# An adaLN block with attention and routed experts: block order, stores of finished sums, and the order of the first loads changed

## The chip, the cores and the metric

One core of a Trainium2 chip runs the whole kernel as one program. The metric is the device time of that core in microseconds (us), the median of three runs; a smaller number is better. The core has a matrix engine (PE; its weight loads are listed as PEld), a vector engine (DVE), an activation engine (ACT), a general engine (POOL) and a queue engine (SP) that mostly issues transfers. Each works through its own list of instructions in order, and they meet at semaphores.

## The reference

The input is `x` of 4 batches of 512 tokens with 256 columns. What is computed, cut to what matters:

```python
mod = (silu(c) @ wmod).reshape(4, 6, 1, 256)
sa, ca, ga, sb, cb, gb = ...            # shift, scale and gate, twice
ga = (2*(ga >= 0) - 1) * maximum(abs(ga), 0.25)   # gb likewise
h = layernorm(x) * (1 + ca) + sa
x = x + ga * attention(h)               # 32 query heads and 8 key heads of width 8, causal
h = layernorm(x) * (1 + cb) + sb
# 16 experts, 4 per token: best 2 of 4 groups of experts, then best 4 in them,
# weights normalized to a sum of 1; one shared expert for every token
ffn = sum_e cw[:, e] * (swiglu(h @ up[e].T) @ down[e].T) + swiglu(h @ sup.T) @ sdown.T
return x + gb * ffn
```

## The kernel before, in words

The program has two parts, `attention()` and `ffn()`, and an order that a small planner in the file makes. `Plan` holds operations, each with an engine, an assumed cost, what it needs, buffers that it takes and gives (`hold`), and a due time. `Plan.next` takes at each step the operation that can start earliest by those costs, the due time breaking ties, and `go` emits its instructions. So the order of each engine's list is fixed when the program is built, and an engine whose next instruction waits holds up all behind it.

**Attention.** Each batch has four packs, each of two key heads with their eight query heads: 16 packs, numbered s. `norm1(b)` (line 666) normalizes a batch, turns it on PE, applies shift and scale on ACT, and calls `split` (725) for the projections of queries and keys. `split` writes each value as a sum of three bf16 parts and stores these to memory (`qd`, `kd`). `load(s)` (808) reads a pack back as `qx` (3 transfers) and `kx` (9 transfers). For packs 0 and 1 the key loads are issued by ACT, otherwise by SP. `unused(n)` (511) fills the three pairs of `qx` and `kx` buffers beforehand, on DVE. `row_max(s)` (834) multiplies queries and keys (L860), adds the mask (L868) and takes row maxima on DVE (L881, 22 units a pack). `shift(s)` (897) splits the maxima, turns them on PE (L920), copies them (`mrow`, L930), and SP writes them into spare rows of `qx` (L940). Only then can `pack(s)` (944) start on the scores (L1001): ACT's exponentials follow (L1013), POOL's causal selection (L1020) and the product with the values (L971). `modulation(b)` (571) makes the gates and the second shift and scale of one batch, spread over all partitions, in two groups of eight PE instructions (L580) with DVE and ACT behind them; there are eight such groups. `later_loads` (1383) fetches batches 1 to 3 of `x` and the weights of the shared expert; `blank_all` (1394) fills two accumulators `acc_d` and the spare rows of `rows_d`.

**Second norm and routing.** `after(b)` (1078) projects the attention's result and adds it to `x`. `norm2(b)` (1146) makes the second norm, the router and for each token four slots; POOL scatters its row into `rows_d`, which has one region for each expert (L1342).

**Experts.** `make_table` (314) makes from the counts of rows a table of at most 79 blocks of 128 rows: the first row of each (`row_i`) and its expert (`of_i`), expert after expert. Several DVE operations there have 79 by 16 elements on each partition (L345 to L369). `shared` (397) does the shared expert (PE L416 and L454), adding into `x_sb`. `block(j)` (1483) fetches 128 rows (SP L1493), turns them (PE L1504), multiplies by the expert's first matrix (PE L1524), then SiLU (ACT L1534) and product (DVE L1538, reading ACT's result), turns back (PE L1543), copies (DVE L1547), multiplies by the second matrix (PE L1552), scales by the row's weight (ACT L1562), and POOL scatters the result with addition into `acc_d[j % 2]` (L1565). `meta` (DVE L1514, L1517) takes the token and the weight of each row, the latter as a sum over 16 columns masked by `is_of`. `read` (388) loads a register from a table (SP and PE, L389).

**End.** When all blocks are planned, eight pairs of tiles of 128 by 512 are read from the two accumulators (L1613, by SP and ACT), added, multiplied by the gate and added to `x_sb` (DVE and POOL, L1618 to L1623), and stored (L1624).

Of the kernel before, what the change touches and what calls it, by code (L numbers as in the profile page):

```python
# [10 lines left out]
F32 = mybir.dt.float32  # L11
BF16 = mybir.dt.bfloat16
AF = mybir.ActivationFunctionType
ALU = mybir.AluOpType
# [22 lines left out]
CAP = B * S + P  # L37
NBLK = B * S * TOPK // P + E - 1
# [113 lines left out]
def kernel(  # L152
# [92 lines left out]
    tile_rows = steps_of("tile_rows", [P, B * NT], [[P, B * NT]])  # L245
    number = steps_of("number", [P, NBLK], [[1, NBLK]])
    expert = steps_of("expert", [P, E], [[1, E]])
    begin = steps_of("begin", [P, E], [[CAP, E]])

    free = const.tile([P, E], F32, name="free")  # L250
    nc.gpsimd.tensor_copy(free, begin)
# [59 lines left out]

    table = {}

    def make_table(pool, needs, due):
        t, n = table, NBLK

        def counts():

            rows = pool.tile([P, E], F32, name="rows", bufs=1)
            nc.vector.tensor_tensor(rows, free, begin, ALU.subtract)  # L320
            full = pool.tile([P, E, B * NT], F32, name="full", bufs=1)
            nc.vector.tensor_tensor(
                full,
                rows.unsqueeze(2).to_broadcast([P, E, B * NT]),
                tile_rows.unsqueeze(1).to_broadcast([P, E, B * NT]),
                ALU.is_gt,
            )
            t["blocks"] = pool.tile([P, E], F32, name="blocks", bufs=1)
            nc.vector.tensor_reduce(t["blocks"], full, AX.X, ALU.add)

        def starts():
            blocks = t["blocks"]
            earlier = pool.tile([P, E, E], F32, name="earlier", bufs=1)
            nc.vector.tensor_tensor(
                earlier, before, blocks.unsqueeze(1).to_broadcast([P, E, E]), ALU.mult
            )
            first = t["first"] = pool.tile([P, E], F32, name="first", bufs=1)
            nc.vector.tensor_reduce(first, earlier, AX.X, ALU.add)
            t["last"] = pool.tile([P, E], F32, name="last", bufs=1)
            nc.vector.tensor_tensor(t["last"], first, blocks, ALU.add)  # L340

        def of():

            t["gone"] = pool.tile([P, n, E], F32, name="gone", bufs=1)
            nc.vector.tensor_tensor(  # L345
                t["gone"],
                t["last"].unsqueeze(1).to_broadcast([P, n, E]),
                number.unsqueeze(2).to_broadcast([P, n, E]),
                ALU.is_le,
            )  # L350
            t["of"] = pool.tile([P, n], F32, name="of", bufs=1)
            nc.vector.tensor_reduce(t["of"], t["gone"], AX.X, ALU.add)

        def is_of():
            t["is_of"] = pool.tile([P, n, E], F32, name="is_of", bufs=1)
            nc.vector.tensor_tensor(
                t["is_of"],
                expert.unsqueeze(1).to_broadcast([P, n, E]),
                t["of"].unsqueeze(2).to_broadcast([P, n, E]),
                ALU.is_equal,  # L360
            )

        def base():

            nc.vector.tensor_tensor(
                t["gone"], t["is_of"], t["first"].unsqueeze(1).to_broadcast([P, n, E]), ALU.mult
            )
            t["row"] = pool.tile([P, n], F32, name="row_f", bufs=1)
            nc.vector.tensor_reduce(t["row"], t["gone"], AX.X, ALU.add)  # L369
            nc.vector.tensor_tensor(t["row"], number, t["row"], ALU.subtract)  # L370

        def rows():

            row, of = t["row"], t["of"]
            nc.vector.tensor_scalar(row, row, float(P), None, ALU.mult)
            nc.vector.scalar_tensor_tensor(row, of, float(CAP), row, ALU.mult, ALU.add)
            nc.vector.tensor_scalar(row, row, float(E * CAP), None, ALU.min)
            nc.vector.tensor_scalar(of, of, float(E - 1), None, ALU.min)
            for name in ("row", "of"):
                t[f"{name}_i"] = pool.tile([P, n], mybir.dt.int32, name=f"{name}_i", bufs=1)  # L380
                nc.vector.tensor_copy(t[f"{name}_i"], t[name])

        op = needs
        for f, cost in ((counts, 0.9), (starts, 0.9), (of, 2.8), (is_of, 1.4), (base, 2.8), (rows, 1.0)):
            op = plan.add("DVE", cost, f, needs=[op], due=due)
        return op

    def read(t, n, engine, top):
        return nc.values_load(  # L389
            t[0:1, n : n + 1],  # L390
# [97 lines left out]
    def attention():  # L488
        with ExitStack() as ectx:
# [21 lines left out]
            def unused(n):  # L511
                nc.vector.memset(kx[n], -1.0)
                nc.vector.memset(qx[n], 0.0)
# [10 lines left out]
            def fill(after_it):  # L524

                filled.append(plan.add("DVE", 2.7, lambda: unused(0), [after_it], -6.5))
                for n, t in enumerate(vaugs):
                    summed.append(
                        plan.add(
                            "POOL", 3.6, on_pool(lambda t=t: denominators(t)), [after_it], n - 6.5  # L530
                        )
                    )
# [8 lines left out]
            plan.free.update(PE=6.5, ACT=5.0, DVE=5.0, POOL=6.0, SP=4.0)  # L541

# [28 lines left out]
            def modulation(b, last, due):  # L571

                st = {}
                h1, h2 = hold("p1"), hold("p1")

                def project(parts):
                    st["p"] = ps1.tile([P, 2, D], F32, name="p1")
                    for w, part in enumerate(parts):
                        for k in range(KC):
                            nc.tensor.matmul(  # L580
                                st["p"][:, w, :],
                                lhsT=sct[:, k, b : b + 1].to_broadcast([P, P]),
# [5 lines left out]
                def sign():  # L588
                    st["sign"] = work.tile([P, 2, D], F32, name="ao")
                    nc.vector.tensor_scalar(st["sign"], st["p"], 0.0, 2.0, ALU.is_ge, ALU.mult)  # L590
                    nc.vector.tensor_scalar_add(st["sign"], st["sign"], -1.0)

                def size():
                    st["size"] = work.tile([P, 2, D], F32, name="ao")
                    nc.vector.tensor_tensor(st["size"], st["p"], st["sign"], ALU.mult)

                def gates():
                    nc.vector.scalar_tensor_tensor(
                        g_sb[:, b], st["size"], 0.25, st["sign"], ALU.max, ALU.mult
                    )  # L600

                def second():
                    nc.scalar.copy(m2_sb[:, b, 0, :], st["p"][:, 0, :])
                    nc.scalar.add(m2_sb[:, b, 1, :], st["p"][:, 1, :], 1.0)

                op = plan.add("PE", 1.7, lambda: project((2, 5)), [last], due(), takes=[h1])
                op = plan.add("DVE", 1.15, sign, [op], due())
# [55 lines left out]
            def any_bank(b):  # L663

                if b > 0:
                    return one_bank()
# [1018 lines left out]
```

## Time and profile before

| what | us |
|---|---|
| median of three runs | 753.69 |
| lowest and highest run | 751.95, 757.3 |
| the profiled execution | 746.31 |
| its span, first to last instruction | 744.4 |
| PE busy in the span | 651.1 |
| DVE busy | 455.6 |
| ACT busy | 317.4 |
| POOL busy | 346.2 |

The mean granted clock of PE was 0.946 of full speed. A profile is of one execution: starts and lengths below are of that one. A line of a chain or a timeline begins with start and length in us. A line by windows gives busy time of PE, PEld, DVE, ACT and POOL (with the number of instructions), then the granted clock of PE, the busy share of the transfer engines and the rate of transfers. A busy PE is not PE at its peak, since matmuls overlap and their ends are modelled; in the chain of work that ended last PE's matmuls appear at the pace at which they follow each other. "SPq" and "ACTq" are transfers being issued by that engine.

### The profile page before, as it was taken

To read this page: it belongs to the slowest core of one execution; us is meant where nothing else is said; L and a number is where in the kernel's file an instruction comes from. 1 tells how busy PE (TensorE), PEld (TensorE's weight loads), DVE (VectorE), ACT (ScalarE), POOL (GpSimd) and SP (SyncE) were. 2 spreads that over 40 slices of the span, in tenths; PEclk is the share of its full clock that TensorE was granted. 3 is DMA by queue.
4 is the path that set the end of the run, shared out by engine and by line. 5 is a ranking of instruction groups with operands and counts; after the bars stand their busy time and mean duration, and the time that the engine had idled before them with its cause. 6 is when DMAs were issued, how large, how long until landed. Compare 5 with 4: busy or idle time off the path is not lost.

```text
span 744.4 us, 12881 instructions
## 1 busy us (share of the span) xinstructions
PE 651.1 (87%) x4205; PEld 411.5 (55%) x4236; DVE 455.6 (61%) x1286; ACT 317.4 (43%) x557; POOL 346.2 (47%) x449
## 2 busy tenths in 40 slices
PE   5576999999999999999987897599999999999920
PEld 3343455555544554445443385488777777777710
DVE  4695868778888888787885056644333333333417
ACT  2103654575556654564655411022444444444400
POOL 4000222335257462673736643722566666556632
PEclk9787999999999999999999799799999999999965
DMA  4585211111133220332101196821576666666575
GB/s 135 128 253 198 72 27 41 42 42 47 29 100 102 65 64 13 108 102 57 42 11 55 63 300 200 205 69 30 96 110 110 109 110 110 102 108 110 66 188 186
DMA packets 54969, 74.51 MB, mean 100 GB/s; under 512 B 8024, under 2 KB 48056, under 8 KB 53752
## 3 DMA queue, kind: packets, MB, share of 16 engines
q1 hardware_dynamic: 37992, 51.99, 25.1%
q0 software_dynamic: 14448, 19.31, 16.0%
q10 hardware_dynamic: 2464, 2.39, 1.1%
q8 instruction: 35, 0.57, 0.3%
q14 instruction: 30, 0.25, 0.1%
HBM read 41.11 MB, written 32.16 MB: 98 GB/s over the span
## 4 chain that ended last, share of the span: by engine, by line
PE 66%; DVE 17%; DMA 6%; POOL 3%; issue 3%; ACT 2%; ACTq 0%; another core or an unknown queue 0%; SPq 0%; DVEq 0%; POOLq 0%
PE pu L1524 13%; PE py L1552 9%; PE pa L971 8%; PE pr L860 8%; PE p L1001 6%; DVE mx_s L881 6%; PE pu L416 5%; PE py L454 3%; PE pr L868 2%; PE pb L1543 2%; PE pt L1504 2%; DMA s<-acc_d 2%; PE p L580 1%; ACT ex L1013 1%; DMA kx<-kd 1%
## 5 line engine op out<-in xcount | busy, mean ns | idle before, releaser
L881 DVE TENSOR_REDUCE mx_s<-pr 128x1 f32<-128x384 f32 (+3 forms) x352 | 212.6, 635 | 52.6 <-PE pr L868 50.5
L1013 ACT ACTIVATE ex<-p 128x1024 f32<-128x1024 f32 (+1 forms) x192 | 163.2, 880 | 103.3 <-PE p L1001 77.4
L1020 POOL TENSOR_SCALAR_AFFINE_SELECT ex<-ex 128x256 f32<-128x256 f32 (+1 forms) x192 | 93.5, 493 | 180.2 <-ACT ex L1013 177.8
L1565 POOL DMA_INDIRECT acc_d<-y_b,token x79 | 123.0, 1556 | 77.2 <-DVE token L1514 32.3
L860 PE MATMUL pr<-kx,qx 125*128 125x384 bf16 (+3 forms) x512 | 125.2, 309 | 20.9 <-DVE mx_s L881 10.0
L1524 PE MATMUL pu<-up_sb,xt 128*128 x316 | 106.6, 460 | 0.0
L1001 PE MATMUL p<-qx,kx 128*128 128x384 bf16 (+3 forms) x481 | 92.0, 299 | 9.5 <-DMA qx<-mrow 6.5
L971 PE MATMUL pa<-ex,vaug 128*32 128x512 f32 (+3 forms) x1024 | 96.8, 450 | 2.5 <-POOL ex L1020 1.0
L860 PEld LDWEIGHTS <-qx 125*128 125x128 bf16 x512 | 47.0, 101 | 77.4 <-issue 49.7
L868 PE MATMUL pr<-seen,ident_h 128*128 128x128 bf16 (+2 forms) x352 | 88.5, 251 | 0.0
L1552 PE MATMUL py<-down_sb,at_b 88*128 x316 | 81.5, 379 | 1.2 <-DVE at_b L1547 1.2
L1342 POOL DMA_INDIRECT rows_d<-row,slot x64 | 64.2, 1003 | 25.7 <-DVE slot L1339 13.0
L1552 PEld LDWEIGHTS py<-down_sb,at_b 88*128 88x128 f32 x316 | 59.7, 189 | 21.9 <-ACT y_b L1562 1.7
L1538 DVE TENSOR_TENSOR a_b<-sg_b,pu 128x176 f32<-128x176 f32 x79 | 26.6, 337 | 71.7 <-ACT sg_b L1534 71.6
L1001 PEld LDWEIGHTS <-kx 128*128 128x128 bf16 x512 | 40.8, 98 | 40.9 <-issue 25.8
L1524 PEld LDWEIGHTS pu<-up_sb,xt 128*128 128x128 f32 x316 | 53.9, 190 | 16.7
L1562 ACT ACTIVATE y_b<-py,cw_b 128x256 f32<-128x256 f32 x79 | 37.4, 473 | 46.5 <-PE py L1552 46.5
L1547 DVE COPY at_b<-pb 88x256 f32<-88x256 f32 x79 | 33.2, 420 | 29.7 <-PE pb L1543 29.7
L1534 ACT ACTIVATE sg_b<-pu 128x176 f32<-128x176 f32 x79 | 25.1, 317 | 60.6 <-PE pu L1524 58.3
L416 PE MATMUL pu<-h2t,sup_sb 128*128 128x256 f32 (+1 forms) x192 | 48.2, 402 | 1.7 <-DVE a L436 1.7
L868 PEld LDWEIGHTS <-ident_h 128*128 128x128 bf16 x352 | 35.0, 99 | 22.8 <-issue 15.7
L416 PEld LDWEIGHTS pu<-h2t,sup_sb 128*128 128x128 f32 (+1 forms) x192 | 36.6, 193 | 9.8 <-DVE a L436 2.0
(176 smaller groups left out, 738.2 us busy)
## 6 DMA issues: line engine op xcount, KB each, us to landing
x<-rows_d SPq DMA_DIRECT2D x79, 136.5 KB
qx<-qd SPq DMA_DIRECT2D x48, 192.0 KB
up_sb<-in_up_t SPq DMA_DIRECT2D x8, 704.0 KB
acc_d<-blank SPq DMA_DIRECT2D x2, 2176.0 KB
qd<-pt SPq DMA_DIRECT2D x16, 192.0 KB
down_sb<-in_down_t SPq DMA_DIRECT2D x8, 352.0 KB
rows_d<-blank SPq DMA_DIRECT2D x17, 136.5 KB
x_sb<-in_x SPq DMA_DIRECT2D x4, 512.0 KB
```

What stands on the lines that cost most here:

```text
L416: nc.tensor.matmul(st["p"][:rows, w, :], lhsT=sup_sb[:, k, c0 : c0 + rows], rhs=h2t[:, k, c1 : c1 + half], start=(k == 0), stop=(k == KC - 1),
L860: nc.tensor.matmul(pr[:, h, :], lhsT=qx[s % 3][:QKZ, REP * j + r + h, ts(i, P)], rhs=kx[s % 3][:QKZ, j, :w], start=True, stop=False, skip_ ...
L868: nc.tensor.matmul(pr[:, :, w - P :], lhsT=ident_h, rhs=seen.unsqueeze(1).to_broadcast([P, n, P]), start=False, stop=True, skip_group_chec ...
L881: nc.vector.tensor_reduce(mx[s][:, i, c0 : c0 + n], st["pr"], AX.X, ALU.max)
L971: nc.tensor.matmul(st["pa"][32 * r : 32 * r + 32, c * P :], lhsT=vaugs[b % 2][:, c, SLOTS * n + j, :], rhs=exs[r], start=(j == 0 and c == ...
L1001: nc.tensor.matmul(pe[:, h, :], lhsT=kx[s % 3][:, j, ts(c, P)], rhs=qx[s % 3][:, REP * j + r + h, c * P :], start=True, stop=True,)
L1013: nc.scalar.activation(ex, st["pe"], AF.Exp, scale=qk_scale)
L1020: nc.gpsimd.affine_select(out=st["ex"][:, :, 0:P], in_=st["ex"][:, :, 0:P], pattern=[[0, n], [1, P]], base=0, channel_multiplier=-1, compa ...
L1342: dma = nc.gpsimd.indirect_dma_start(out=rows_d, out_offset=bass.IndirectOffsetOnAxis(ap=st["slot"][:, i, k : k + 1], axis=0), in_=st["row ...
L1524: nc.tensor.matmul(st["pu"], lhsT=st["xt"][:, k, :], rhs=up_sb[:, bass.ds(st["e"], 1), k, :].rearrange("p e f -> p (e f)"), start=(k == 0) ...
L1552: nc.tensor.matmul(st["py"], lhsT=st["at"][:, c, :], rhs=down_sb[:, bass.ds(st["e"], 1), c, :].rearrange("p e d -> p (e d)"), start=(c == ...
L1565: nc.gpsimd.indirect_dma_start(out=acc_d[j % 2], out_offset=bass.IndirectOffsetOnAxis(ap=st["token"][:, 0:1], axis=0), in_=st["y"], in_off ...
```

## The change

1. The start. `norm1` projects keys before queries and stores the first pack's keys first. The norm of batch 1 is planned directly behind batch 0's, before the first maxima, and takes the (still unused) score banks; its part of `x` is loaded at the start. The fills of `qx` and `kx` go from DVE to POOL. Keys of pack 1 are loaded by SP instead of ACT.
2. The gates. One `modulations` for all four batches, on 4 rows, in two groups of eight PE instructions as the profile counts them; the result goes to memory and is read back spread over all partitions (2 transfers of 1 MB). It is planned after the maxima of pack 0, and `later_loads` after those of pack 1; `blank_all` after those of pack 3.
3. `shift` issues the transfer of the maxima from ACT's queue, not SP's.
4. Blocks are numbered by the batch in which the first row of the block lies, then by expert. `make_table` works with one block on each partition: 25 small DVE instructions.
5. `meta` reads the block's expert into a DVE register and copies that one column, in place of the masked sum. The buffers of tokens go from 6 to 12, those of `y_b` from 5 to 8.
6. `end(b)`: when the last block that can hold rows of batch b is scattered, the sums of that batch are read, finished on DVE in six instructions between the blocks (each placed right behind a `copy_back`) and stored; so for batches 0 to 2. The scatters do not wait for these loads. Only batch 3 is left for the end, in four tiles of 128 by 256, on DVE alone.

Built, PE's list has before the first scores: batch 0's norm, batch 1's norm and projections, all of pack 0's maxima, and 38 of the 108 PE instructions (weight loads counted) of pack 1's. Before the change it had 64 of these 108, two groups of turns of batch 1, and no projection of it. On ACT's list the nine loads of pack 0's keys stand behind the first shift-and-scale of batch 1.

```diff
@@ make_table
-            t["gone"] = pool.tile([P, n, E], F32, name="gone", bufs=1)
-            nc.vector.tensor_tensor(
-                t["gone"],
-                t["last"].unsqueeze(1).to_broadcast([P, n, E]),
-                number.unsqueeze(2).to_broadcast([P, n, E]),
-                ALU.is_le,
-            )
...
+            gone, of, last = small("gone", [P, B * E]), small("of_v", [P, 1]), t["last"]
+            nc.vector.tensor_scalar(gone, last, number, None, ALU.is_le)
+            nc.vector.tensor_reduce(of, gone, AX.X, ALU.add)
...
@@ unused, fill
-                nc.vector.memset(kx[n], -1.0)
-                nc.vector.memset(qx[n], 0.0)
+                return [nc.gpsimd.memset(kx[n], -1.0), nc.gpsimd.memset(qx[n], 0.0)]
...
@@ modulation -> modulations
-                                lhsT=sct[:, k, b : b + 1].to_broadcast([P, P]),
+                                lhsT=sct[:, k, :],
...
+                def spread():
+                    nc.sync.dma_start(out=m_d, in_=mods)
+                    for t, at in ((g_sb, 0), (m2_sb, 2)):
+                        nc.sync.dma_start(
+                            out=t, in_=m_d[:, at : at + 2, :].unsqueeze(0).to_broadcast([P, B, 2, D])
+                        )
...
@@ norm1
+                    (wk_sb, NG * HD, kd, NPK * b, NPK, SLOTS),
                     (wq_sb[:, :, ts(0, P)], P, qd, NPK * b, n, PH),
-                    (wk_sb, NG * HD, kd, NPK * b, NPK, SLOTS),
...
@@ load
-                    engine, queue = ("SP", nc.sync) if s > 1 else ("ACT", nc.scalar)
+                    engine, queue = ("SP", nc.sync) if s > 0 else ("ACT", nc.scalar)
@@ shift
-                    "SP", 0.4, lambda: nc.sync.dma_start(out=qx[s % 3][QKZ:], in_=st["mrow"]),
-                    [op], due, gives=[mrow_hold],
+                    "ACT", 0.1, lambda: nc.scalar.dma_start(out=qx[s % 3][QKZ:], in_=st["mrow"]),
+                    [op], due, lag=2.5, gives=[mrow_hold],
@@ the plan of attention()
             norm1(0, Pace(-8.0, -4.0, 40))
-            filled += [
-                plan.add("DVE", 2.7, lambda n=n: unused(n), [stored[False, 0]], -3.0)
-                for n in (1, 2)
-            ]
             load(0)
+
+            norm1(1, Pace(-4.0, -1.6, 42))
             load(1)
-            later = plan.add("SP", 5.0, later_loads, [loaded[0][-1]], 0.0, lag=8.0)
-            plan.add("SP", 3.0, blank_all, [later, loaded[1][-1]], 1.0)
-            gates_made = loaded[1][-1]
-            due = Pace(0.5, 3.0, B * 6)
-            for b in range(B):
-                gates_made = modulation(b, gates_made, due)
             row_max(0)
             row_max(1)
+
+            gates_made = modulations(placed[0], placed[1], 1.5)
+            later = plan.add("SP", 4.0, later_loads, [placed[1]], 1.6, lag=8.0)
...
+                if s == 1:
+                    plan.add("SP", 3.0, blank_all, [placed[3]], 3.0)
@@ block
+            def which():
+                st["e_v"] = read(t["of_i"][j : j + 1, 0:1], DVE, E - 1)
+
...
-                junk = fp.tile([P, E], F32, name="junk")
-                nc.vector.tensor_tensor_reduce(
-                    junk, x[:, D + 1 :], t["is_of"][:, j, :], 1.0, 0.0, ALU.mult, ALU.add, st["cw"]
-                )
+                nc.vector.tensor_copy(st["cw"], x[:, D + 1 :][:, bass.ds(st["e_v"], 1)])
...
+                tc.declare_no_dep(dma.ins, group="sums", reason="finished rows")
@@ new: end(b, n, due), for batches 0 to 2
+            needs = [*puts[n - 2 : n], backs[n + 3]]
+            pace = iter(backs[n + 8 :])
...
+                    nc.vector.tensor_tensor(st[0], st[0], st[1], ALU.add)
...
+                    nc.vector.tensor_tensor(
+                        st[0], st[0], g_sb[:, b, 1:2, :].to_broadcast([P, half, D]), ALU.mult
+                    )
...
+                    nc.vector.tensor_tensor(st[0], st[0], x_sb[:, tiles, :], ALU.add)
...
+                op = plan.add("DVE", 0.81, add, [*op, next(pace)], due, gives=holds[1:])
+                op = plan.add("DVE", 1.05, gate, [op, next(pace)], due)
+                op = plan.add("DVE", 0.7, residual, [op, next(pace)], due)
+                plan.add("SP", 0.5, store, [op], due, lag=4.0, gives=holds[:1])
@@ the end of ffn()
-        for n in range(B * NT // half):
-            pair = [ep.tile([P, half, D], F32, name=f"s{n}_{i}") for i in range(2)]
+        for n in range((B - 1) * NT, B * NT):
+            pair = [ep.tile([P, D], F32, name=f"s{n}_{i}") for i in range(2)]
...
-            eng = nc.gpsimd if n % 2 == 0 else nc.vector
-            eng.tensor_tensor(s, s, x_sb[:, ts(n, half), :], ALU.add)
-            nc.sync.dma_start(out=out_r[:, ts(n, half), :], in_=s)
+            nc.vector.tensor_tensor(s, s, g_sb[:, B - 1, 1, :], ALU.mult)
+            nc.vector.tensor_tensor(s, s, x_sb[:, n, :], ALU.add)
+            nc.sync.dma_start(out=out_r[:, n, :], in_=s)
```

## The prediction

> **What bounds the kernel now.** I read the windows by stage first, then the chain of work that ended last inside each, then single timelines.
>
> ```profile
> core 0: us, PE busy (x) PEld busy (x) DVE busy (x) ACT busy (x) POOL busy (x), PEclk, DMA share, GB/s
> 31.00:67.80 36.80, 25.23 (x123) 15.28 (x124) 28.14 (x60) 4.07 (x6) 1.04 (x1) 0.78 0.84 256
> 67.80:422.00 354.20, 337.96 (x2729) 174.68 (x2759) 270.81 (x643) 201.37 (x272) 166.96 (x272) 0.99 0.20 55
> 422.00:474.00 52.00, 36.31 (x176) 29.58 (x177) 32.87 (x101) 6.93 (x16) 25.69 (x28) 0.86 0.75 228
> 501.00:713.20 212.20, 210.39 (x1007) 160.03 (x1005) 78.50 (x404) 92.83 (x240) 125.60 (x84) 1.00 0.61 95
> 713.20:744.40 31.20, 0.00 (x0) 0.00 (x0) 17.12 (x20) 0.00 (x0) 7.72 (x6) 0.50 0.70 210
> ```
>
> Two stages are PE's: attention from the first scores on (338 of 354 us busy) and the blocks (210 of 212). There only less PE work or a new wait moves the end. The other three have other limits: the start, the routing and the end, where PE does nothing for 31.2 us. The chain names these limits:
>
> ```profile
> 61.62 6.10 DMA qx<-mrow
> 70.75 1.72 PE p L734 x4
> 133.30 1.73 PE p L580 x8
> 469.48 1.48 DVE row_f L369
> 603.37 0.86 PE py L1552 x4
> 604.24 0.22 PE pb L1543 x2
> 604.46 0.22 PE pt L1504 x2
> 604.68 1.19 PE pu L1524 x4
> 722.97 6.11 DMA s<-acc_d
> ```
>
> The first scores wait for a transfer of 6.10 us; PE also does batch 1's projections and the gates inside attention; a DVE operation of 1.48 us ends the table; a block is PE alone, 0.86 + 0.22 + 0.22 + 1.19 = 2.49 us, 79 times; the end is loads of sums and DVE.
>
> **Start.** Row maxima of pack 0 begin at 31.0 (PE) and the first scores at 67.8; between, PE is busy 25.2 of 36.8 us at a clock of 0.78. The transfer that ends the wait was slow because the fills came just before on the same queue:
>
> ```profile
> 52.10 2.74 SPq L1396 DMA_DIRECT2D acc_d<-blank  x2
> 54.94 6.59 SPq L1400 DMA_DIRECT2D rows_d<-blank  x1
> ```
>
> After the change the fills are planned after pack 3's maxima, and the maxima leave on ACT's queue. Pack 0's keys now stand behind the first shift-and-scale of batch 1 on ACT, so I put the first row maxima at 33, 2 us later than now. They take 22 DVE units, 13.3 us (212.6 us over 16 packs), plus about 2.8 for four other DVE operations of batch 1's norm at 0.69 and 3.8 for its projections on PE: to 53. Splitting and turning the maxima about 1.6, their copy 0.57, issue 0.76 (SP's median) and landing about 2.0 (an estimate from small transfers outside the fills): scores at 58.2, -9.6 us. Bounds -5 (keys 5 us later still) to -13. Batch 1's extra 0.5 MB of `x` at the start is about 1.5 us at the 350 GB/s of the first loads, which end near 10; transfers are idle from 10 to 20, so it costs nothing unless the first weights wait behind it, then 1.5.
>
> **PE work leaving attention.** Batch 1's projections, 1.72 + 1.86 + 1.72 + 1.93 (L734 three times, L789 once) = 7.2, move before the first scores. Of eight gate groups five stood after 67.8 at about 1.74; two remain, so 3 x 1.74 = 5.2 go. Against that, 64 of the 108 PE instructions of pack 1's maxima were done before the scores and now 38: 0.24 of 4.7 us (10% of the chain over 16 packs), +1.1. Sum -11.3. At the least -8, if PE waits where this work stood.
>
> **Transfers that pile up.** The spread of the gates (2 MB) and `later_loads` (about 2.4 MB) stand on SP just ahead of the last three key loads of pack 3, `blank_all` (4.4 MB) ahead of the last loads of pack 5. Now 67.8 to 422 moves only 55 GB/s. At 256 GB/s the first pile is 17 us, the second 17; a pack's PE time is about 22, and maxima run about a pack ahead. I take +5 of 0 (loads that far ahead) to +10 (one pile half bare). Issuing the maxima on ACT holds its exponentials 0.76 us, 16 times = 12.2; ACT is busy 201 of 354, so I count +2, bounds -1 (PE waited 6.5 us in all for this transfer) to +5. The fills of `qx` on POOL precede its first selection and are hidden there; bare they are about 2 us. Attention after 67.8: -11.3 + 5 + 2 = -4.3.
>
> **Table.** L345 to L369 run 461.2 to 472.4, 11.2 us, and PE waits for it:
>
> ```profile
> 473.24 1.22 PE L454 MATMUL py<-sdown_sb,a 96*128 96x256 f32 x2 [8.98 <-DVE a L436]
> ```
>
> `a` is an ordinary DVE product queued behind the table. The new table is 25 operations, no larger than 128 by 64; neighbouring operations of that size pace 0.25 and of 128 by 16 0.20: 13 x 0.25 + 12 x 0.20 = 5.65. So -5.6, and PE's 9 us wait lets it through; bounds -4 and -7.
>
> **Blocks.** PE's list per block is unchanged. DVE gets two things. First, reading the expert into a DVE register, in place of the masked sum (0.16 + 0.08). DVE loads no register from a table now; the nearest rows are those of PE and SP:
>
> ```profile
> L389 SPq TENSOR_LOAD <-row_i x79: 262/270/547, 477.4 to 686.9; - x79
> L389 PEldq TENSOR_LOAD <-of_i x79: 296/302/572, 490.2 to 702.2; - x79
> ```
>
> Second, 18 operations of `end` behind a `copy_back`, 0.69 each alone. The room for them:
>
> ```profile
> 603.76 0.34 DVE L1538 TENSOR_TENSOR a_b<-sg_b,pu 128x176 f32<-128x176 f32 x1 [1.18 <-ACT sg_b L1534]
> 604.50 0.42 DVE L1547 COPY at_b<-pb 88x256 f32<-88x256 f32 x1 [0.40 <-PE pb L1543]
> ```
>
> From the copy's end (604.92) the next product could start at 606.25: 1.33; PE's turn came 0.14 after the product's end, so 1.47 in all. Into it go meta's 0.23, the load 0.30 and in 18 blocks 0.69: 1.22. The load is short and hidden; if it drains DVE, what is late is the next product, then `pb` on PE. The Trainium skill ("DMA: Bandwidth & Descriptors", Latency and other measured facts) gives a floor of about 0.6 us for such a load; the two rows here show half. By the rule end-op blocks need 0.69 + 0.23 + 0.60 = 1.52, over by 0.05: 18 x 0.05 = 0.9 us; by the row nothing. From below it is 0, since PE paces; from above, the load's dependency (the DVE register use) is unknown. I take +1 of 0 to +6. SP now issues the loads of sums and stores too: 12 + 6 issues at up to 0.92 (a fetch unthrottled) within 212 us, against a fetch that runs several blocks ahead: nothing, or about one block, 2.5, if a fetch is late. The larger pools only loosen waits.
>
> A rule speaks against `end`: the skill ("SBUF — State Buffer", Who interferes with whom) says that a DVE instruction with two SBUF inputs and a POOL instruction that reads SBUF keep each other out for the whole instruction. The end of the run agrees, POOL's scatter does not:
>
> ```profile
> 729.79 1.63 DVE L1619 TENSOR_TENSOR s<-s,g_sb 128x512 f32<-128x512 f32 x1
> 649.08 1.56 POOL L1565 DMA_INDIRECT acc_d<-y_b,token  x1 [1.73 <-DVE a_b L1538]
> 649.72 0.16 DVE L1517 CUSTOM_DVE_ANT_0 junk<-x,is_of 128x16 f32<-128x16 f32 x1
> ```
>
> Beside POOL's addition, L1619 takes 1.63 and not 0.69; but L1517, two SBUF inputs, took its usual 0.16 in the middle of a scatter. By the rule each end operation would take about 1.69: (1.69 + 0.23 + 0.30 - 1.47) x 18 = +13.5; by the row 0. I take the row, and keep the rule as a rival.
>
> **End.** Now: last scatter issued 713.90 to 715.45, SP's loads issued at 717.74, first sum 722.93, last DVE operation over at 740.87, end 744.4 (3.5 for the store). Four times less has to be loaded: 1 MB, landed about 2.5 after issue (an estimate; 6.11 for the first of 4 MB), so 720.2. Twelve DVE operations of 128 by 256 at 0.40 (0.69 halved, plus start) = 4.8, no POOL beside them: 725.0, store 3.3: 728.3. That is -16; bounds -14 to -18.5.
>
> **Sum.** -9.6 - 4.3 - 5.6 + 1 - 16 = -34.5. The span goes from 744.4 to about 709.9. The profiled run took 746.31, 1.9 more than its span, and the median shown, 753.69, is 7.4 above that run. I take this distance as unchanged and subtract from the median: 719.
>
> **Rivals.** *B, attention gives it all back:* batch 1's norm ahead of the first maxima makes the keys late, or the piles stop PE at packs 3 and 5. For it: the keys' place on ACT's list, 8.8 MB moved into a dense stage. Against: 55 GB/s there now. Then only end, table and blocks count: 753.7 - 16 - 5.6 + 1 = 733. *C, end operations shut out by the scatter,* as priced above: 719 + 13.5 = about 732. For it the 1.63 row, against it the 0.16 row. *D, on the other side: the register load on DVE.* The windows have 1.47 - 0.23 = 1.24 us for it in every block. If DVE must empty and fetch before the copy that uses the register, a load of L costs (L - 1.24) x 79. It eats the whole gain at 1.24 + 34.5/79 = 1.68 us; at 2.0 it costs 60: 779. For it: no DVE load is in the trace[...]. Against: 0.27 and 0.30 on two other engines. *E, all pays in full:* piles and ACT's issue cost nothing, the start gives 13: about 707.
>
> **How the numbers follow.** Forecast 0.60, B 0.17, C 0.07, D 0.12 (a third within 1%, the rest slower), E 0.04. About 1% (7.5 us) is what a measurement of this kernel can tell from no change. Faster by over 1% is the forecast, B, C and E: 0.88; within 1% 0.04; slower 0.08. The forecast's own range is 707 to 731, its bounds added in part; 705 to 738 takes in B and C and leaves out D and the far ends of B and E, about 2 in 10.
>
> **What would show it.** In the changed kernel's profile: the first L1040 scores near 58 (start); a window from there to the last pack some 4 us shorter than 354, with PE's waits for `kx` and `qx` loads at packs 3 and 5 of at most 5 us; PE's wait for `a` near 3 rather than 9; a block still at 2.49 us on the chain, with DVE's register load near 0.3; L1660 and L1663 at 0.7 between blocks; 15 us from the last block's PE work to the end rather than 31. Wrong would be a row maximum that starts after 38, a DVE load over 1.2 us, block intervals over 2.55, or a chain in attention that runs through transfers.

## The result and the profile after

| | before | after |
|---|---|---|
| median, us | 752.55 (20 runs) | 759.6 (20 runs) |
| ratio | 1 | 1.0118, interval 1.0088 to 1.0149 |
| the profiled execution | 746.31 | 763.72 |
| its span | 744.4 | 762.0 |

Slower by 1.2%; forecast was 719. The two profiled executions lie 6 under and 4 over their medians, so the 17.6 us between their spans overstates the 7 us between the medians. The stages below come from these single executions; what a change is worth is taken from the ratios of the experiments. (Ratios and intervals leave disturbed runs out.)

The windows of the changed kernel, cut at its own first row maxima, first scores, end of attention, first all-block stretch and last PE work:

```profile
core 0: us, PE busy (x) PEld busy (x) DVE busy (x) ACT busy (x) POOL busy (x), PEclk, DMA share, GB/s
37.80:64.35 26.55, 20.60 (x98) 10.95 (x97) 21.12 (x39) 5.11 (x9) 0.00 (x0) 0.74 0.32 80
64.35:441.70 377.35, 335.61 (x2688) 167.71 (x2720) 270.68 (x639) 196.11 (x260) 167.90 (x272) 0.96 0.26 74
441.70:531.00 89.30, 72.45 (x303) 57.66 (x304) 38.31 (x137) 11.06 (x27) 35.24 (x41) 0.83 0.54 165
531.00:740.90 209.90, 208.69 (x1001) 158.98 (x999) 85.64 (x346) 93.27 (x240) 123.42 (x82) 1.00 0.66 118
740.90:762.00 21.10, 0.03 (x1) 0.00 (x0) 4.83 (x12) 0.47 (x1) 5.79 (x4) 0.59 0.49 103
```

| stretch | before | after | difference | predicted |
|---|---|---|---|---|
| to the first scores | 67.8 | 64.35 | -3.4 | -9.6 |
| first scores to the last pack's result | 354.1 | 377.35 | +23.2 | -4.3 |
| from there to PE's last work | 290.7 | 299.2 | +8.5 | -4.6 |
| PE's last work to the end | 31.8 | 21.1 | -10.7 | -16 |

Attention is where most of the time went. PE is busy there 335.6 us of 377.35, against 338 of 354.1 before: its idle time rose from 16.1 to 41.7 us, and the work that is left, less than before, ran at a mean granted clock of 0.96 (0.99 before) and took nearly as long. The chain of work that ended last now runs through transfers there:

```profile
83.43 3.35 DMA qx<-mrow
92.38 3.66 SPq L1425
98.17 8.36 DMA sdown_sb<-in_sdown_t
133.80 4.98 DMA qx<-mrow
141.70 6.95 SPq L1437
152.46 3.75 DMA kx<-kd
```

L1425 is in `later_loads`, L1437 in `blank_all`. On SP they stand ahead of the last three key loads of packs 3 and 5, which are issued from 101.6 and from 150.0 on. PE's waits between 64 and 165 us name what came of it (line, what it waited for, us in total, times, longest):

```profile
PE pr L898 <- DMA sdown_sb<-in_sdown_t: 6.3, 1, 6.3
PE pr L898 <- DMA kx<-kd: 4.3, 1, 4.3
```

L898 makes row maxima, and reads no `sdown_sb`: the wait is put down to a transfer that stood ahead of its keys. The first wait is for pack 3's keys, the second for pack 5's; the expectations below count them as packs 2 and 4. Pack 3's first products stand on PE's list in the midst of pack 1: when the wait begins, at 100.3, a quarter of pack 1's scores is still to come behind them. The start, on ACT's timeline:

```profile
29.21 2.25 ACTq L860 DMA_DIRECT2D kx<-kd  x6
31.51 0.78 ACT L710 ACTIVATE ht<-p,mod_t 128x512 f32<-128x512 f32 x1 [1.60 <-DMA kx<-kd]
40.44 0.58 ACT L765 CAST pt<-p 128x512 bf16<-128x512 f32 x1 [5.51 <-DMA kd<-pt]
```

ACT's key loads hold the second shift-and-scale of batch 1 for 1.60, and ACT then waits 5.51 for a store of keys to land before it can write another `pt`. PE's first product for row maxima comes at 37.8; DVE takes its first maximum at 41.66, behind a subtraction that waited for this `pt`, 3.8 us after PE (1.05 before). The first scores come at 64.35.

### The profile page after: what moved, and what is told of

Same layout as the page of the kernel before. It is cut to its first block, busy times and chain, and to the rows that moved or that the text cites. A ratio compares the mean times of both kernels' runs of the same rounds, so it can differ in the third digit from the quotient of the medians.

```text
span 762.0 us, 12858 instructions
## 1 busy us (share of the span) xinstructions
PE 661.2 (87%) x4155; PEld 407.5 (53%) x4188; DVE 439.0 (58%) x1206; ACT 314.9 (41%) x551; POOL 355.0 (47%) x450
## 4 chain that ended last, share of the span: by engine, by line
PE 63%; DVE 16%; DMA 8%; issue 4%; SPq 3%; POOL 3%; ACT 3%; ACTq 0%; DVEq 0%; POOLq 0%
PE pu L1558 12%; PE py L1586 9%; PE pa L1010 7%; PE pr L898 7%; DVE mx_s L919 6%; PE pu L416 5%; PE p L1040 5%; PE py L454 3%; PE pr L906 3%; PE pt L1538 2%; PE pb L1577 2%; DMA qx<-mrow 2%; PE p L1161 2%; ACT ex L1052 2%; DMA acc_d<-y_b,token 2%
## 5 line engine op out<-in xcount | busy, mean ns | idle before, releaser
L1599 POOL DMA_INDIRECT acc_d<-y_b,token x79 | 124.8, 1580 | 84.2 <-DVE token L1551 26.1
L898 PE MATMUL pr<-kx,qx 125*128 125x384 bf16 (+3 forms) x512 | 126.5, 311 | 22.4 <-DVE mx_s L919 8.9
L1040 PE MATMUL p<-qx,kx 128*128 128x256 bf16 (+3 forms) x479 | 93.3, 302 | 11.2 <-DMA qx<-mrow 7.5
L898 PEld LDWEIGHTS <-qx 125*128 125x128 bf16 x512 | 46.9, 102 | 84.0 <-issue 60.9
L1381 POOL DMA_INDIRECT rows_d<-row,slot x64 | 62.6, 979 | 25.8 <-DVE slot L1378 13.1
L416 PE MATMUL pu<-h2t,sup_sb 128*128 128x256 f32 (+1 forms) x192 | 52.6, 430 | 9.1 <-issue 5.4
L416 PEld LDWEIGHTS pu<-h2t,sup_sb 128*128 128x128 f32 (+1 forms) x192 | 38.6, 205 | 18.8 <-issue 5.8
```

What stands on the lines that cost most here:

```text
L416: nc.tensor.matmul(st["p"][:rows, w, :], lhsT=sup_sb[:, k, c0 : c0 + rows], rhs=h2t[:, k, c1 : c1 + half], start=(k == 0), stop=(k == KC - 1),
L898: nc.tensor.matmul(pr[:, h, :], lhsT=qx[s % 3][:QKZ, REP * j + r + h, ts(i, P)], rhs=kx[s % 3][:QKZ, j, :w], start=True, stop=False, skip_ ...
L1040: nc.tensor.matmul(pe[:, h, :], lhsT=kx[s % 3][:, j, ts(c, P)], rhs=qx[s % 3][:, REP * j + r + h, c * P :], start=True, stop=True,)
L1381: dma = nc.gpsimd.indirect_dma_start(out=rows_d, out_offset=bass.IndirectOffsetOnAxis(ap=st["slot"][:, i, k : k + 1], axis=0), in_=st["row ...
L1599: dma = nc.gpsimd.indirect_dma_start(out=acc_d[j % 2], out_offset=bass.IndirectOffsetOnAxis(ap=st["token"][:, 0:1], axis=0), in_=st["y"], ...
```

## The experiments

Theory A: attention's own changes make the loss, above all the transfers moved onto SP's queue. Rival R: the experts' side makes it. Ratios are to the kernel before, with intervals; milestones in us are of each kernel's profiled execution.

**Which half.** `e1_old_attention` keeps only the parts 4 to 6 of the change, `e2_old_experts` only the parts 1 to 3. `e3_fills_early` is the changed kernel with

```diff
             load(1)
+            later = plan.add("SP", 5.0, later_loads, [loaded[0][-1]], 0.0, lag=8.0)
+            plan.add("SP", 3.0, blank_all, [later, loaded[1][-1]], 1.0)
             row_max(0)
...
-            later = plan.add("SP", 4.0, later_loads, [placed[1]], 1.6, lag=8.0)
...
-                    plan.add("SP", 3.0, blank_all, [placed[3]], 3.0)
```

and `e4_no_register`, which has no operation that loads the register, with

```diff
-                nc.vector.tensor_copy(st["cw"], x[:, D + 1 :][:, bass.ds(st["e_v"], 1)])
+                nc.vector.tensor_copy(st["cw"], x[:, D + 1 : D + 2])
```

> Attention as before the change, table, blocks, sums and end as after it. Theory A (the loss is made in attention, where the span after stands 20 us behind when the last pack ends, and the experts' side gains a little: 31.2 to 22.7 at the end, 6 given back between attention and the first blocks): 2 to 8 us under the kernel before, ratio 0.990 to 0.998. Rival R (the loss is made on the experts' side by DVE's register loads, the slow queues around 490 to 505 and late scatters): over the kernel before, ratio 1.005 or more.

> Attention as after the change, table, blocks and end as before it. Theory A: attention ends some 20 us later than before, ratio 1.020 to 1.030, end of 31 us as before. Rival R: 0.985 to 1.000.

> The changed kernel, but later_loads and blank_all planned behind the first key loads as before the change; all else as changed. Theory A1 (the two piles on SP's queue at packs 2 and 4, 6.3 and 4.3 us of PE waiting for keys and the lower clock after them, are the main part of the loss in attention): 10 to 17 us under the changed kernel, ratio to the kernel before 0.990 to 1.000, attention's end about 428 rather than 442. Rival A2 (the start and ACT's queue make the loss): ratio 1.008 to 1.02, since the fills now delay the keys and the first maxima.

> The changed kernel without the register load on DVE: the weight of a row is copied from a fixed column, so each row is weighted by the first expert's weight rather than its own expert's. Theory A: as the changed kernel, ratio to the kernel before 1.006 to 1.014, since PE paces the blocks. Rival R (the DVE loads stall SP, PE and ACT around 490 to 505, 10 us): ratio 0.995 to 1.003, SP's 16 fills of blank rows back at 15 us from 26.

| kernel | ratio | first scores | last pack | PE's last work | span |
|---|---|---|---|---|---|
| before | 1 | 67.8 | 421.9 | 712.6 | 744.4 |
| after | 1.0118 | 64.35 | 441.7 | 740.9 | 762.0 |
| e1 | 0.9881 (0.9836 to 0.9926) | 67.2 | 419.7 | 716.4 | 738.4 |
| e2 | 1.0279 (1.0225 to 1.0334) | 64.6 | 442.1 | 738.5 | 771.9 |
| e3 | 0.9924 (0.9901 to 0.9947) | 65.4 | 424.9 | 718.3 | 739.2 |
| e4 | 1.0131 (1.0084 to 1.0177) | 64.3 | 439.9 | 737.5 | 759.0 |

The experts' half is faster by 1.2%, attention's half slower by 2.8%. R falls; leaving out the register load gains nothing. Putting the moved transfers back gives 1.0118 - 0.9924 = 1.9%, about 14.6 us. In the two profiles the packs shrink by 17.9 us with the same PE work in them. The row of e3:

```profile
65.40:424.90 359.50, 329.10 (x2688) 165.40 (x2720) 269.87 (x638) 196.20 (x260) 168.02 (x272) 0.99 0.24 72
```

PE is idle 30.4 us there and not 41.7, and busy 6.5 us less, at a clock of 0.99 and not 0.96. So about a third of what the piles cost goes with a lower clock: between 100 and 120 us, around the first wait, it is 0.75 in the changed kernel and 1.00 in e3.

**What is left in attention.** e3 still needs 359.5 us from first scores to last pack, 354.1 before, though less PE work is in it. `e5_maxima_on_SP` is e3 with the maxima on SP's queue, `e7_gates_in_one` is e1 with `modulations` in place of the four `modulation`.

```diff
-                    "ACT", 0.1, lambda: nc.scalar.dma_start(out=qx[s % 3][QKZ:], in_=st["mrow"]),
-                    [op], due, lag=2.5, gives=[mrow_hold],
+                    "SP", 0.4, lambda: nc.sync.dma_start(out=qx[s % 3][QKZ:], in_=st["mrow"]),
+                    [op], due, gives=[mrow_hold],
```

> The kernel of e3_fills_early with the maxima issued on SP's queue again. In e3 attention still takes 359.5 us from first scores to last pack against 354.1 before, with 30 us of PE idle against 16, part of it waits for the maxima (5.7) and for POOL's selections behind them (4.7). Theory A3 (ACT's queue makes the maxima late): 4 to 8 us under e3, ratio to before 0.982 to 0.988. Rival A4 (the PE work taken out was the filler at the ends of packs, so the waits come whatever the queue): within 2 us of e3, ratio 0.990 to 0.996.

> The kernel of e1_old_attention with only the gates of the change: one modulations for all batches, planned behind the key loads of pack 1 as the first gates were before. It takes 6 groups of PE, about 10 us, out of attention. Theory A4 (PE work in attention is filler, the chain of maxima paces it): e1 within 3 us, ratio 0.985 to 0.992. Rival A5 (attention is bound by PE, each us of PE work counts): 5 to 10 us under e1, 0.975 to 0.982.

Measured: e5 1.0020 (1.0000 to 1.0040), e7 0.9959 (0.9939 to 0.9979), both outside every expectation on the slow side. The milestones say why: first scores at 76.4 in e5 and 75.9 in e7. In e5 the maxima of pack 0 stand on SP behind the fills, in e7 2 MB of gates came on top of them. What was to be tested shows behind that: e5's packs take 354.0, 5.5 less than e3's; e7's 348.8 (75.9 to 424.7) against e1's 352.5, 3.7 less. Of e1's eight gate groups five, about 1.74 us each, lie in this stretch, of e7's none: 8.7 us less work. So it seems that the maxima on ACT gain at the first pack and lose at the others. `e12_only_first_on_ACT` is e3 with

```diff
-                    "ACT", 0.1, lambda: nc.scalar.dma_start(out=qx[s % 3][QKZ:], in_=st["mrow"]),
-                    [op], due, lag=2.5, gives=[mrow_hold],
+                    "ACT" if first else "SP", 0.1 if first else 0.4,
+                    lambda: queue.dma_start(out=qx[s % 3][QKZ:], in_=st["mrow"]),
+                    [op], due, lag=2.5 if first else None, gives=[mrow_hold],
```

where `first` is `s == 0` and `queue` ACT's for it, SP's otherwise.

> The kernel of e3_fills_early with the maxima of pack 0 on ACT's queue, all later ones on SP's. e3 has first scores at 65.4 and 359.5 us of packs, e5 76.4 and 354.0. Theory Q (ACT's queue helps only where fills stand on SP's, and costs 5.5 us in the packs): both gains, 5 to 6 us under e3, ratio to before 0.983 to 0.987. Rival (the packs' length follows from when they start): e3 within 2 us, 0.990 to 0.995.

0.9785 (0.9748 to 0.9823): 1.4% under e3, about 10 us, twice what was expected. First scores 64.9, packs 348.3, against 359.5. PE's waits in the packs, of e3 and then of e12:

```profile
PE p L1040 <- DMA qx<-mrow: 6.5, 7, 1.9
PE pa L1010 <- POOL ex L1059: 4.7, 6, 0.9
```

```profile
PE p L1043 <- DMA qx<-mrow: 2.7, 3, 1.0
PE pa L1013 <- POOL ex L1062: 1.7, 2, 1.2
```

11.2 us over 15 packs is 0.75 each; one issue holds ACT 0.73 to 0.76. The sizes agree, but `lag=2.5` also changes the planner's order, and no run tells ACT's time from that order. (e13 and e14 below have the attention of e12 and a third fill. Their packs take 352.9 and 352.1, with one wait of 4.9 and 3.2 for pack 1's maxima, which stand on SP behind the fills; but for that wait they agree with e12.)

**The end.** `e6_all_sums_last` is e1 with all sums read at the end, as before. `e8_three_sums` is e1 with a third accumulator:

```diff
-                    out=acc_d[j % 2],
+                    out=acc_d[j % 3],
```

with the third load and addition that it needs in `end` and at the end.

> The kernel of e1_old_attention with the sums of all four batches read and finished at the end, as before the change; table and blocks as changed. Theory A: the end goes back from 22 to 31 us and scatters no longer fall behind (5 us); e1 plus 5 to 10 us, ratio to before 0.996 to 1.002. Rival (loads and stores between blocks gave nothing net): e1 within 2 us, 0.986 to 0.991.

> The kernel of e1_old_attention with three accumulators in turn rather than two, so that a scatter waits for the third before it. In e1 the last scatter is issued 6.9 us after PE's last work. Theory S (the wait for the scatter two before makes the lag): last scatter within 2.5 us of PE's last work, 3 to 5 us under e1, less about 1 for a third load and addition at the end: ratio 0.982 to 0.986. Rival (POOL's own 1.56 us and the transfers' rate make it): e1 or up to 2 us over, 0.988 to 0.992.

e6: 1.0045 (1.0024 to 1.0067), 1.6% over e1, and 31.7 us from PE's last work to the end against 22.0: `end` is worth about 12 us, a little over what was expected. In e6 the last scatter follows its row's weighting by 0.9 us, in the changed kernel it comes 5.7 late. The last scatter of the changed kernel (POOL) and the weighting that it belongs to (ACT):

```profile
740.97 0.47 ACT L1596 ACTIVATE y_b<-py,cw_b 128x256 f32<-128x256 f32 x1 [1.45 <-PE py L1586]
747.17 1.56 POOL L1599 DMA_INDIRECT acc_d<-y_b,token  x1 [0.76 <-DMA acc_d<-y_b,token]
```

The same two in e8:

```profile
722.82 0.47 ACT L1562 ACTIVATE y_b<-py,cw_b 128x256 f32<-128x256 f32 x1 [1.67 <-PE py L1552]
723.57 1.55 POOL L1565 DMA_INDIRECT acc_d<-y_b,token  x1 [0.58 <-ACT y_b L1562]
```

The row of the changed kernel names the releaser: an earlier scatter. In the chain a scatter starts 4.85 us after the one before it on the same accumulator (735.61 to 740.46, of which the transfer takes 4.09), and two blocks take 4.98: a lag, once there, is hardly made up. It grew each time sums were loaded: from 0.3 to 1.8 at 642, from 0.8 to 4.5 at 685, from 4.0 to 5.9 at 726. (The kernel before lags by up to 2.8, and by 0.8 at its end.) With three accumulators the lag is 0.3 and the end takes 18.6. e8 as a whole is 0.9958 (0.9938 to 0.9978), over e1: its third fill, 2.2 MB, again stands on SP ahead of the first maxima, and the first scores come at 74.4. So theory S holds and the expected ratio doesn't. `e10_first_maxima_ACT` is e8 with the edit of e12, `e11_gates_and_ACT` adds the gates in one.

> The kernel of e8_three_sums with the maxima of pack 0 alone issued on ACT's queue, all later ones on SP's. In e8 the first scores are at 74.4, behind three fills on SP, and the last scatter no longer lags (0.3 us). Theory Q (the fills ahead on SP's queue hold the first maxima): first scores at 62 to 64, packs as long as in e1, end of 18.6 us, so 5 to 8 us under e1: ratio 0.977 to 0.982. Rival (the fills hold the transfer itself, whichever queue issues it): first scores at 72 or later, ratio 0.990 to 0.996.

> The kernel of e10_first_maxima_ACT with the gates of all batches in one, as in e7_gates_in_one. There the first scores came 8.8 us later behind the 2 MB of gates on SP's queue, and the packs took 3.8 us less. Theory Q: with the first maxima on ACT the delay is gone, 3 to 4 us under e10, ratio 0.972 to 0.978. Rival (the 2 MB still delay the fills and key loads of pack 2): e10 or up to 4 us over.

e10: 0.9787 (0.9747 to 0.9828), first scores 64.4. The fills ahead on the queue had held the maxima. Whether fills beside it would slow the transfer is not tested: e10's first fill starts on SP at 64.44, when the maxima have landed, after 2.82 us as in the changed kernel. e11: 0.9803 (0.9762 to 0.9844), nothing gained: first scores at 60.3, but PE then waits 7.3 us for pack 1's maxima, on SP behind the fills and the gates, and packs end at 419.4 against 418.4. The number is the rival's; the wait is for maxima, not for the keys that it named.

**The table.** In the changed kernel PE's wait at the table is 2.25 and not 9.0, but another of 5.42 follows, and SP's 16 fills of blank rows take 26.15 us where before they took 15.08:

```profile
488.21 0.72 PE L454 MATMUL py<-sdown_sb,a 96*128 96x256 f32 x2 [2.25 <-DVE row_i L381]
500.76 3.73 PE L416 MATMUL pu<-h2t,sup_sb 128*96 128x256 f32 x8 [5.42 <-issue]
483.26 26.15 SPq L1505 DMA_DIRECT2D rows_d<-blank  x16
```

`e9_long_table` is e1 with the table made long again, `e14_fills_after_puts` is `e13_all_together` with SP's first fill outside the group of transfers that need not wait for each other, so that it waits for the last scatter of rows, and planned behind it.

```diff
+            pad = small("pad", [P, 632])
+            nc.vector.tensor_copy(pad, number.to_broadcast([P, 632]))
+            for _ in range(7):
+                nc.vector.tensor_tensor(pad, pad, pad, ALU.max)
```

> The kernel of e1_old_attention with eight further DVE operations of 128x632 at the end of the table, about 5.7 us, that touch only a tile of their own: the table is again as long as before. Theory G (what the short table gains is given back, since in e1 PE waits 2.9 us at the table and then 2.7 and 5.2 in the next 20 us while SP's queue steps in 0.7 us, in all 18 us idle after attention as before the change): e1 within 2 us, ratio 0.986 to 0.992, PE idle after attention 16 to 19. Rival (the table's end sets the first block): e1 plus 4 to 6 us, 0.993 to 0.998.

> The kernel of e13_all_together, but the first of the 16 fills of blank rows waits until the last scatter of rows has landed, and the second for the first. Theory F (fills and scatters issued side by side, with DVE free, make SP's queue step in 0.7 us and hold PE 2.7 and 5.2): SP's fills take 15 us rather than 25, no waits of PE over 2.5 us for what is not a product, PE idle between attention and the first block 5 us less; first fetch about 10 us later, still under shared work of PE; 0 to 5 us under e13. Rival (something else holds the queues, such as PE, ACT and DVE working beside the scatters): PE waits as in e13, and the later first fetch costs 0 to 8 us.

e9: 0.9851 (0.9801 to 0.9900), not slower than e1; PE waits 9.06 at the table, nothing over 2.3 after it, and is idle 18.5 us between attention and the first block (e1: 18.2); SP's fills take 16.31. So against e1 the short table's gain was given back in full. (The planner was told of the longer table, so the order differs too.) In ten profiles of experiments with the short table, and in that of the changed kernel, SP's fills took 24.6 to 26.2 us. In the changed kernel SP's instructions, register operations of 0.04 us among them, came 0.70 apart for some 15 us, and ACT starts at 499.42 on a product that PE had finished at 495.34. But in three others the fills took about 15: e13, e14 and `e15_late_loads_only`, whose experts' part is the changed kernel's, unaltered. The fills of e15 and e13:

```profile
480.23 15.06 SPq L1504 DMA_DIRECT2D rows_d<-blank  x16
```

```profile
461.90 14.86 SPq L1507 DMA_DIRECT2D rows_d<-blank  x16
```

From the last pack to PE's last work these three take 286.6 to 287.4 us. The stretch in the kernel before, the changed kernel and e15:

```profile
421.90:712.60 290.70, 273.70 (x1302) 212.42 (x1302) 123.00 (x536) 104.58 (x267) 161.88 (x125) 0.97 0.62 121
441.70:740.90 299.20, 281.14 (x1302) 216.64 (x1302) 123.94 (x482) 104.32 (x267) 158.66 (x123) 0.95 0.63 132
438.60:725.20 286.60, 275.37 (x1302) 213.23 (x1302) 123.75 (x482) 104.46 (x267) 158.24 (x123) 0.98 0.68 138
```

PE is idle 17.0 us before, 18.1 in the changed kernel, 11.2 in e15 (17.9 to 19.9 in all eleven that step). So the short table took 5.8 us of waiting away where SP did not step, and nothing where it did. Of the 8.5 us by which the changed kernel is longer here 7.4 are not waiting: the same number of PE instructions is busy for 281.1 us and not 273.7, at a clock of 0.95 and not 0.97. A lower clock comes without the stepping, too: e2, with the old table and fills of 15.48, is busy 277.8 us at 0.96. Why it was granted lower is not shown.

Since e13 has no stepping either, e14 (0.9721, 0.9687 to 0.9755) can't tell theory F from its rival. What makes the queues step stays open: DVE's register loads are excluded (e4 steps without them), and the instructions alone don't decide it. One rival stands untested: e13 to e15 ran on a chip on which no other experiment ran, and the ten that step ran on two others.

**Which pile, and the sum.** e13 is e12 with the three accumulators of e8. e15 is the changed kernel with `blank_all` alone back at the start.

> The kernel of e12_only_first_on_ACT with the three accumulators of e8. e12 has PE's last work at 710.8, the last scatter 5.9 us later, and the end 21.5 us after PE. Theory S (the wait for the scatter two before): no lag, end 18 us after PE, 2 to 4 us under e12: ratio 0.973 to 0.977. Rival: the third accumulator's fill delays the start again, e12 or over, 0.978 or more.

> The changed kernel with blank_all alone back at the start; gates' spread and later_loads stay behind pack 1's maxima. It tells the two piles apart. Theory A1: each pile is about half: the wait of 6.3 us at pack 2 stays, that of 4.3 at pack 4 goes, with its clock loss 7 to 9 us under the changed kernel, ratio 1.000 to 1.005. Rival (the second pile was harmless, the first is all): 1.008 to 1.013.

e13: 0.9689 (0.9653 to 0.9725), 723.33 against 746.08 us: no lag of scatters, 17.8 us of end. It is the fastest here, and better than expected because of the queue that didn't step; its third fill cost the 4.9 us at pack 1 named above, as its rival had it in kind. e15: 0.9945 (0.9922 to 0.9969), under both expectations for the same reason, so its ratio doesn't tell the piles apart. Its profiled execution, 7 us over its median, still has a wait of 7.9 for the keys of pack 3, none for those of pack 5, and ends the last pack at 438.6: its packs are 3 us shorter than the changed kernel's, against 18 with both piles back (e3). By that one profile the gates' spread and `later_loads` are the costly pile. Most of the 1.7% between e15 and the changed kernel is the stretch after the packs, 12.6 us shorter. Had the changed kernel had that, too, it would have come to about 747 (an estimate: 759.6 - 12.6), close to the kernel before and still far from 719.

## Why the prediction was wrong

The step that failed is attention: forecast at -4.3, it came to +23.2. Its terms were +5 for the piles, +2 for ACT's issues and -11.3 for PE's work; the packs of the profiles give +17.9 (e3 to the changed kernel), +11.2 (e12 to e3) and -5.8 for what remains (before to e12). One sign of being wrong that the prediction named came true: a chain in attention that runs through transfers.

- **"Transfers that pile up ... I take +5".** This failed first. The place was right, the keys of packs 3 and 5 (waits of 6.3 and 4.3 us), and the bound of +10 was too low: 14.6 us by the ratios. Of the 17.9 us in the profiles 11.3 are waiting; the other 6.5 are the same PE work at a lower clock, for which no term stood. I weighed 17 us of transfer against a pack of 22 and took maxima to run a pack ahead. But pack 3's first products stand on PE's list before the last quarter of pack 1's scores, and a pack's maxima are finished hardly ahead of their use: in e3 those of pack 1 are copied at 85.4, 3 us before pack 0's result. PE takes its list in order, so a late key is then a late score.
- **"Issuing the maxima on ACT ... I count +2".** About 10 us by the ratios: nearly the 12.2 us of issues in full, though it is not shown that it is ACT's time and not the other order. Of the 6.5 us that PE had waited for this transfer 5.0 were the first scores', which the start had counted already. The gain at the first pack was right in kind and is the part worth keeping.
- **"PE work leaving attention ... -11.3".** A busy share of 95% was read as "PE alone sets the pace". With the piles and ACT's later issues out of the way (e12) the packs take 348.3 and not 354.1: -5.8. Against e10, which has the old start and old gates, PE has 8.1 us less to do in e12 and is idle 17.2 us and not 14.7: some of the work had filled waits. e7 alone got 3.7 of 8.7. The packs of e12 and e10:

```profile
64.90:413.20 348.30, 331.10 (x2721) 166.01 (x2720) 271.10 (x638) 195.19 (x259) 167.47 (x273) 0.99 0.26 74
64.40:418.30 353.90, 339.19 (x2764) 174.45 (x2763) 271.63 (x644) 202.10 (x273) 166.77 (x272) 1.00 0.26 74
```

- **Start, -9.6.** -3.4. Row maxima of pack 0 started at 37.8 on PE, not 33, and at 41.66 on DVE. The keys behind ACT's shift-and-scale were foreseen; not that ACT would wait 5.51 for `pt`, nor that fills on POOL would slow the norm on DVE (below). No run takes these two apart.
- **Table, -5.6.** In waiting it came, -5.8, where SP's queue did not step; where it did, in eleven profiles of fourteen with the short table, all was given back. That, and the busy time that grew by 7.4 us at a lower clock, was in no bound of mine. (The 11.2 us are the whole table's, L320 to L381; L345 to L369 alone are 7.5.)
- **Blocks.** Right: blocks at 2.49 us, the register load at 0.32, end operations at 0.68 between blocks, so the row and not the rule was to be taken both times.

```profile
L389 DVEq TENSOR_LOAD <-of_i x79: 305/318/757, 489.1 to 725.3; - x79
L1663 DVE TENSOR_TENSOR s<-s,g_sb x6: 676/678/679, 645.8 to 732.9; 128x512 f32<-128x512 f32 x6
```

- **End, -16.** -10.7. The loads and the twelve operations were right (753.75 to 759.0 on DVE). Missing was what loads of sums between the blocks do to the scatters: each set them back, and 4.85 us from one scatter to the next on the same accumulator, within 4.98 for two blocks, left no room to catch up. At the end that is a lag of 5.7 us. e6, without these loads, has 0.9, e8 takes it away.

Rival B ("attention gives it all back") was the nearest; it should have been allowed to end slower than before, and its price, 733, took attention's loss to be no more than attention's gain.

## What to carry to other kernels

A transfer moved out of an idle start into a dense stage has to be priced by what stands behind it on its queue, at the point where the reader runs least ahead; that lead must be read in the trace, not assumed. The same edit can gain at one place and lose at fifteen others (the first maxima on ACT's queue and all later ones): split it before judging it. Work that is taken from the busiest engine counts only as far as it did not fill a wait, here about half (5.8 us of 11.3, 3.7 of 8.7). And before a stage's longer time is put down to waits, its busy time and clock are to be compared, too.

## What the runs showed of the hardware

POOL's fills hold up DVE. On DVE's timeline of the changed kernel, and POOL's beside it:

```profile
11.21 2.41 DVE L572 TENSOR_SCALAR mod_t<-mod_t 128x8 f32<-128x8 f32 x1
24.00 0.68 DVE L769 TENSOR_TENSOR rest<-pr,pt 128x512 f32<-128x512 f32 x1
24.60 3.90 DVE L653 TENSOR_SCALAR xn<-x_sb,mv,rs 128x256 f32<-128x256 f32 x3
9.94 3.64 POOL L512 MEMSET qx<- 128x4096 bf16 x1
23.29 3.65 POOL L512 MEMSET qx<- 128x4096 bf16 x1
```

An operation of 128 by 8 took 2.41 us and ended with the fill (0.17 in the kernel before). Three of 128 by 256 took 3.90 together, where one takes 0.40 elsewhere in the same norm; the first of them, 2.48 us long, ended 0.15 us after the fill. L769, a `tensor_tensor` inside the same fill, took its usual 0.68. The Trainium skill ("SBUF — State Buffer", Who interferes with whom) says that DVE's `tensor_scalar` can enter a mode that shuts POOL out and is shut out by it, for the whole instruction; these rows agree. Against POOL's scatters no such thing showed: of the 18 end operations, all `tensor_tensor`, three lie wholly inside a scatter and took 0.68.

Second, SP's queue can step in intervals of 0.70 us for some 15 us, with ACT starting 4 us late beside it, while POOL's scatters keep their pitch of 1.27; instructions that had the steps in one profile had none in another.
